# Attention's q and k stacks turned in one transpose per half and laid out by SBUF transfers, with the long fills spread over the steps

## The chip, the cores and the metric

One core of a Trainium2 chip. The metric is the device time of one execution in microseconds (us); smaller is better. Engines are named as in the profile: PE (matmul; PEld is its weight load), DVE, ACT, POOL, and SP, which here does little but issue DMA transfers from its queue.

## What is computed

A sandwich of two residual layers over x of shape (4, 1024, 256), f32:

```python
x = x + layernorm(attention(layernorm(x)))   # 16 heads of 16, rotary q and k, full softmax
x = x + layernorm(moe(layernorm(x)))         # 8 experts of width 684, 2 per token, silu gating
```

In attention q and k are projected, get a bias and rotary embedding, and `softmax(q k^T / 4) v` goes through an output projection. In the second layer each token goes to two of eight experts, chosen by its distance to eight centroids.

## The kernel before, in words

**Order of the work.** Attention is cut into 4 batches (b) x 4 groups of four heads (g) x 2 halves of 512 queries (qb): 32 units of 8 key blocks, 256 *steps* in all. A step (`step`, L720) takes one key block of one unit: the scores of four heads (`sc`, L737), less the rows' maxima by a second matmul into the same bank (L744), exp on ACT (L748), and the product with v of the step before (`av`, L813). The maxima of a unit that comes up to 12 steps later are drawn beside it: `pm` matmuls (L655), each reduced on DVE (L659). Everything else (norms, projections, splits, stacks, output projections, the choice of experts) is cut into small `Work`s (from L402). A planner at build time keeps a clock for each of PE, DVE, ACT and POOL (`free`), places Works by due step where their stated costs fit ("P430 A550" is 430 ns of PE and 550 ns of ACT), at most two PE works a step. The order so made is fixed on PE, DVE, ACT and SP (`manual_schedule`), and POOL's is the program's. What an engine waits for stalls all that stands behind it.

**Stacks.** Scores need near-f32 accuracy from matmuls that take the narrower type fp32r. So a value is split into hi = fp32r(value) and lo = value - hi. The product of a head is one matmul over 64 rows: q holds [hi, lo, hi, lo], k holds [hi, lo, lo, hi], 16 rows each. For each group and each half of 512 tokens, `rotated` (L542, POOL) applies bias and rotary embedding to q and k; `split_up` (L566) writes the split with all four copies (per q and k: a cast, a subtraction, two copies); `stack` (L587) turns it: for each pair of heads and for q and k, four 128x128 transposes (L596) fill one PSUM bank (tile `ps`), and ACT copies it (L603) into the tile that the matmuls read. That is four banks a half and group, 128 in all. In the first group DVE does the second half's split and k's copies. All the first group's splits and stacks come before its maxima, and those before step 0 (end of `sandwich`). `plan_stacks` (L1028) gives the due steps; `all_maxima` (L1020) finishes a group's stacks before its first maxima.

**Fills.** Two DRAM areas are prepared during attention: `rows` (tokens by expert), filled with an empty pattern from the tile `empty` by 35 transfers of 1032 KB (L285), and `wall` (each expert's weights in one block), by 88 DRAM-to-DRAM transfers (L303 to L312). All are issued on SP's queue at the start, behind the first loads. `biases_by_chunk` (L229, due step 54) adds biases to `wall` through small tiles (`flat`, `lin`, `lined`). Settled tokens are scattered into `rows` by POOL from L1000, and the expert stage reads both (L1170, L1178). `resid` stores (L860) are on SP's queue as well.

In SP's instructions each transfer waits for the one eight before it, because there are eight completion semaphores in turn.

Of the kernel before, what the change touches and what calls it, by code (L numbers as in the profile page):

```python
# [8 lines left out]
F32 = mybir.dt.float32  # L9
# [48 lines left out]
def sandwich(  # L58
# [22 lines left out]
    def bank(name, pool=ps1):  # L81
        return pool.tile([P, TB], F32, tag="bank", name=name)
# [155 lines left out]
    def biases_by_chunk():  # L238

        yield "P200 A400 W5000"  # L240
        pc = bank("plin", pssc)
        n = NE * NF
        for i in range(2):
            nc.tensor.transpose(pc[:n, i * FP : (i + 1) * FP], natural[:, i, :], ident[:FP, :FP])
        flat = cl.tile([n, 2, FP], F32, tag="eq", name="flat")
        nc.scalar.copy(flat, pc[:n, : 2 * FP].rearrange("p (i f) -> p i f", i=2))
        for i in range(2):
            nc.sync.dma_start(
                out=lin[i].rearrange("e (f p) -> (e f) p", p=FP), in_=flat[:, i, :]
            )  # L250
        lined = cl.tile([2 * NE, FF], F32, tag="oT", name="lined")
        nc.sync.dma_start(out=lined, in_=lin.rearrange("i e f -> (i e) f"))
        yield "P900 A800"
        pc = bank("pbias_", pssc).rearrange("p (f i) -> p f i", i=2 * NE)
        for f in range(NC + 1):
            m = P if f < NC else FR
            nc.tensor.transpose(
                pc[:m, f, :], lined[:, f * P : f * P + m], ident[: 2 * NE, : 2 * NE]
            )
        biases = cl.tile([P, NE, 2, NC + 1], F32, tag="gt", name="biases")  # L260
        pool.memset(biases, 0.0)
        for f in (slice(0, NC), slice(NC, NC + 1)):
            m = P if f.start < NC else FR
            nc.scalar.copy(
                biases[:m, :, :, f].rearrange("p e i f -> p i e f"),
                pc[:m, f, :].rearrange("p f (i e) -> p i e f", i=2),
            )
        nc.sync.dma_start(
            out=wall[:, :, OB:OR].rearrange("e p w -> p e w"),
            in_=biases.rearrange("p e i f -> p e (i f)"),  # L270
        )
# [7 lines left out]
    for i in range(NTS):  # L279
        nc.gpsimd.tensor_scalar(  # L280
            empty[:, :, i, C + 1], part_id.to_broadcast([P, NTB]), float(2 * B * T + i * P), None,
            ALU.add,
        )
    for i in range(NROW // (NTB * TS)):
        nc.sync.dma_start(  # L285
            out=rows[i * NTB * TS : (i + 1) * NTB * TS, :].rearrange(
                "(n i p) c -> p n i c", p=P, i=NTS
            ),
            in_=empty,
        )  # L290

    wall = tc.dram_tile([NE, P, WW], F32, name="wall")
    lin = tc.dram_tile([2, NE, FF], F32, name="lin")
# [3 lines left out]
    for e in range(NE):  # L297
        for w, to, cols in (
            (wg, 0, slice(0, FF)), (w1, FF, slice(FF - (P - R2), FF)), (w1, FF + P - R2, slice(0, NC * P))
        ):  # L300
            n = cols.stop - cols.start
            for k in range(KC):
                nc.sync.dma_start(  # L303
                    out=wall[e, :, k * WK + to : k * WK + to + n], in_=w[e, k * P : (k + 1) * P, cols]
                )
        nc.sync.dma_start(
            out=wall[e, :, O2:OB].rearrange("p (f c) -> p f c", f=NC),
            in_=w2[e, : NC * P].rearrange("(f p) c -> p f c", p=P),
        )
        for r in (0, R2):  # L310
            nc.sync.dma_start(out=wall[e, r : r + FR, OR:], in_=w2[e, NC * P :])
            nc.sync.dma_start(out=wall[e, r + FR : r + FR + 1, OR:], in_=b2[e : e + 1, :])  # L312
    token_id = const.tile([P, NTB], F32, tag="token_id", name="token_id")
    nc.gpsimd.tensor_scalar(token_id, tiles_at[:, :NTB], float(P), part_id, ALU.mult, ALU.add)

# [247 lines left out]
        e.tensor_tensor(flat, flat, sw.rearrange("p t h s d -> p (t h s d)"), ALU.add)  # L563
        return c

    def split_up(b, g, half, c, e):  # L566
        sp_ = ep2.tile([P, NTB, 2, 4, 4, HD], F32R, tag="split", name=f"split_{b}_{g}_{half}")
        for i in range(2):
            full = c[:, :, 4 * i : 4 * i + 4]
            at = lambda n: sp_[:, :, i, :, n, :]  # L570
            e.tensor_copy(at(0), full)
            e.tensor_tensor(at(1), full, at(0), ALU.subtract)
            e.tensor_copy(at(2), at(i))
            e.tensor_copy(at(3), at(1 - i))
        return sp_

    splits = {}

    def split(b, g, half, fast=False):

        e = nc.vector if fast and half else pool
        yield "G5500"
        c = rotated(b, g, half, e)
        yield "G4000"
        splits[b, g, half] = split_up(b, g, half, c, e)

    def stack(b, g, half, fast=False):  # L587

        for pr in range(2):
            for is_k in range(2):  # L590
                yield "P430 A550"
                if (half, pr, is_k) == (0, 0, 0):
                    stacks[b, g] = stack_tiles(b, g)
                ps = bank(f"ps_{b}_{g}_{pr}_{is_k}_{half}", pssc).bitcast(F32R)
                for t in range(NTB):
                    nc.tensor.transpose(  # L596
                        ps[:, t * P : (t + 1) * P],
                        splits[b, g, half][:, t, is_k, 2 * pr : 2 * pr + 2].rearrange(
                            "p h n d -> p (h n d)"
                        ),  # L600
                        ident_r,
                    )
                (nc.vector.tensor_copy if fast and is_k else nc.scalar.copy)(  # L603
                    stacks[b, g][pr][is_k][:, half * TB : (half + 1) * TB], ps
                )

    def stack_tiles(b, g):
        if (b, g) == groups[-1]:

            both = [  # L610
                ap1.tile([P, 2, T], F32R, tag=f"turned{pr}", name=f"stack_{b}_{g}_{pr}")
                for pr in range(2)
            ]
            return [[m[:, is_k] for is_k in range(2)] for m in both]
        return [
            [
                ap2.tile([P, T], F32R, tag=f"stack{i}", name=f"stack{i}_{b}_{g}_{pr}", bufs=6)
                for i in range(2)
            ]
            for pr in range(2)  # L620
        ]
# [98 lines left out]
    def step(n):  # L720
# [6 lines left out]
        if kb == 0:  # L727
            shifts[u].finish()
        es = []

        def scores(pr):
            q, k_ = stacks[b, g][pr]
# [74 lines left out]
    def weighted(u, kb, es):  # L807
        b, g, qb = order[u]
        if kb == 0:
            avs[u] = psav.tile([P, TB], F32, tag="av", name=f"av_{u}")  # L810
        av = avs[u]
        for j in range(4):
            nc.tensor.matmul(  # L813
                av[32 * j : 32 * j + 32, :], v_aug[kb][:, 4 * g + j, :], es[j],
                start=(kb == 0), stop=(kb == NT - 1),
            )
        free["P"] += 1200
        if kb == NT - 1:
            outputs(u, av)
# [200 lines left out]
    def all_maxima():  # L1020
        for u, (b, g, qb) in enumerate(order):
            for half in range(NQB):
                stacking[b, g, half].finish()
            yield from maxima(u)

    tops = all_maxima()

    def plan_stacks():  # L1028
        for k, (b, g) in enumerate(groups):
            for h in range(NQB):  # L1030
                deps = []
                if k:
                    deps.append(stacking[(*groups[k - 1], h)])
                if k == 1:
                    deps.append(Work(project(0, h, range(NTB), 1), -1))
                if g == 0 and b:
                    preparing[b, h] = Work(
                        prepare(b, h), drawing[b, g] - 22 + 6 * h,
                        after=[splitting[(*groups[k - 1], h)]]
                        + ([preparing[b, 0]] if h else []),  # L1040
                    )
                    deps.append(preparing[b, h])
                splitting[b, g, h] = Work(
                    split(b, g, h, fast=k == 0), drawing[b, g] - (16 if g == NG - 1 else 6), after=deps
                )
            for h in range(NQB):


                deps = [splitting[b, g, i] for i in range(NQB) if i == h or k == len(groups) - 1]
                stacking[b, g, h] = Work(  # L1050
                    stack(b, g, h, fast=k == 0), drawing[b, g] - 1,
                    after=deps + ([stacking[b, g, 0]] if h else []),
                    start=(k - 2) * ITS if 2 < k < len(groups) - 1 else 0,
                )
# [278 lines left out]
    with tc.manual_schedule(engines={ET.SP, ET.PE, ET.DVE, ET.Activation}):  # L1333
# [34 lines left out]
                    first = Work(first_tiles(), n, after=[settling[divmod(NA - 1, NQB)]])  # L1368
        while waiting:
            weighted(*waiting.pop(0))  # L1370
        backs[-1].finish()
        first.finish()
        make_room()
# [128 lines left out]
```

## Time and profile before

| | us |
|---|---|
| median of 3 runs | 1696.88 (1693.59 to 1699.7) |
| the profiled execution | 1706.47, its span 1704.7 |
| first transposes of stacks (L596) | at 36.5 |
| first maxima (L655) | at 42.4 |
| step 0 (first `sc`) | at 84.0 |
| last exp of attention (L748) | at 1079.1 |
| PE waiting for POOL's split, whole run | 16.8, longest 9.1 |
| granted PE clock, mean | 0.969 of full |

A line of the page names engine, operation, output<-inputs, shape and count, then busy time. Where one row stands for a tile, three numbers are the lowest, median and highest duration in ns. PE's times are pipelined and their ends modelled: a busy PE need not be at its peak. In the SP rows a duration is that of the issuing instruction, not of the transfer.

### The profile page before, as it was taken

Reading aid. Unit: us, or ns where it says so; the run is one execution under the profiler, and the core shown is the slowest. Engines: PE = TensorE matmul, PEld = TensorE weight load, DVE = VectorE, ACT = ScalarE, POOL = GpSimd, SP = SyncE. Lnnn points to the kernel's source line nnn. Section 1 sums busy time; section 2 is a strip of 40 time slices with the busy share of each in tenths; the row PEclk is TensorE's granted clock in tenths of the full one; section 3 lists DMA queues with packets and bytes.
Section 4 is the critical chain, followed back from the end, with each engine's and each line's share of the span. In section 5 each row is a group of like instructions: output and inputs, shape, how many; then the busy total and the mean of one; then the engine's idle time right before and its main releaser. Section 6 shows DMA issues by size and latency. Waiting matters only on the chain. (4 is left out here: it accounts for less than half of the span.)

```text
span 1704.7 us, 27788 instructions
## 1 busy us (share of the span) xinstructions
PE 1572.2 (92%) x9704; PEld 1028.0 (60%) x9704; DVE 1059.9 (62%) x2543; ACT 888.4 (52%) x1815; POOL 559.5 (33%) x1101
## 2 busy tenths in 40 slices
PE   3799999999999998999998999999999999999960
PEld 3454555654555554455554444688888888888850
DVE  6576788787788786778777786244334433333338
ACT  2266777676777776678676766522221111222213
POOL 5662344164393344475243121223131111111100
PEclk8999999999999999999999999999999999999985
DMA  8999810101000001000001013164455455777755
GB/s 247 302 300 254 227 45 6 36 26 38 1 26 13 26 13 51 1 26 14 22 5 38 1 38 128 59 217 176 169 209 193 164 208 217 256 282 282 285 202 212
DMA packets 92031, 213.77 MB, mean 125 GB/s; under 512 B 11469, under 2 KB 71092, under 8 KB 86004
## 3 DMA queue, kind: packets, MB, share of 16 engines
q1 hardware_dynamic: 81972, 182.49, 32.5%
q0 software_dynamic: 8768, 25.33, 4.4%
q10 hardware_dynamic: 1152, 4.19, 0.6%
q8 instruction: 76, 1.25, 0.3%
q14 instruction: 63, 0.52, 0.1%
HBM read 148.75 MB, written 80.58 MB: 135 GB/s over the span
## 5 line engine op out<-in xcount | busy, mean ns | idle before, releaser
L659 DVE TENSOR_REDUCE part<-pm 128x1 f32<-128x512 f32 x1024 | 642.0, 683 | 173.1 <-PE pm L655 158.9
L748 ACT ACTIVATE e<-sc 128x512 f32<-128x512 f32 x1024 | 530.3, 604 | 145.5 <-PE sc L744 136.2
L1210 PE MATMUL pu<-xT,w 128*128 128x256 f32 (+3 forms) x2024 | 361.5, 332 | 4.2 <-DMA w<-wall 1.3
L1216 ACT ACTIVATE sil<-pu,w 128x256 f32<-128x256 f32 (+3 forms) x276 | 117.0, 424 | 431.4 <-PE pu L1210 400.5
L1210 PEld LDWEIGHTS pu<-xT,w 128*128 128x128 f32 (+1 forms) x2024 | 313.8, 189 | 37.2 <-issue 5.1
L655 PE MATMUL pm<-stack,stack 64*128 64x512 f32 x960 | 276.7, 466 | 16.6 <-DVE part L659 13.7
L813 PE MATMUL av<-e,v 128*32 128x512 f32 x2048 | 277.5, 614 | 0.0
L744 PE MATMUL sc<-shift,bring 64*128 64x512 f32 x1024 | 232.1, 403 | 3.0 <-ACT shift L644 2.9
L1221 DVE SCALAR_TENSOR_TENSOR h<-pu,w,sil 128x256 f32<-128x256 f32 (+1 forms) x230 | 97.1, 423 | 218.5 <-ACT sil L1216 212.5
L737 PE MATMUL sc<-stack,stack 64*128 64x512 f32 x960 | 221.9, 411 | 5.4 <-issue 3.5
L655 PEld LDWEIGHTS pm<-stack,stack 64*128 64x128 f32 x960 | 133.3, 186 | 136.8 <-DVE part L659 87.2
L1257 POOL DMA_INDIRECT res<-yo,ids x71 | 68.7, 968 | 411.4 <-DVE yo L1256 409.0
L1244 PE MATMUL pe<-w,h 128*128 128x256 f32 x710 | 169.6, 386 | 0.0
L1244 PEld LDWEIGHTS pe<-w,h 128*128 128x128 f32 x710 | 131.0, 190 | 31.2 <-issue 15.2
L737 PEld LDWEIGHTS sc<-stack,stack 64*128 64x128 f32 x960 | 116.6, 187 | 37.6 <-ACT stack L603 8.4
L744 PEld LDWEIGHTS sc<-shift,bring 64*128 64x128 f32 x1024 | 111.4, 188 | 22.4 <-ACT shift L644 7.5
L603 ACT CAST stack<-ps 128x512 fp32r<-128x512 f32 x124 | 72.6, 593 | 47.5 <-PE ps L596 43.9
L596 PEld LDWEIGHTS ps<-ident_r,split 128*128 128x128 f32 x512 | 53.1, 145 | 72.7 <-ACT e L748 31.0
L1256 DVE TENSOR_SCALAR yo<-pe,xt 128x256 f32<-128x256 f32 x71 | 34.3, 484 | 100.3 <-PE pe L1244 100.3
L596 PE MATMUL ps<-ident_r,split 128*128 128x128 f32 x512 | 69.9, 268 | 16.8 <-POOL split L326 16.8
L1000 POOL DMA_INDIRECT rows<-xr,to x64 | 62.8, 981 | 68.3 <-DVE to L995 43.8
L813 PEld LDWEIGHTS av<-e,v 128*32 128x32 f32 x2048 | 40.5, 108 | 72.2 <-issue 69.6
(296 smaller groups left out, 1479.3 us busy)
## 6 DMA issues: line engine op xcount, KB each, us to landing
w<-wall SPq DMA_DIRECT2D x46, 2034.0 KB
rows<-empty SPq DMA_DIRECT2D x35, 1032.0 KB
xt<-rows SPq DMA_DIRECT2D x25, 258.0 KB
wall<-in_wg_dram SPq DMA_DIRECT2D x16, 342.0 KB
wall<-in_w_dram SPq DMA_DIRECT2D x16, 320.0 KB
wall<-in_w_dram SPq DMA_DIRECT2D x8, 640.0 KB
xb<-in_x_dram POOLq DMA_DIRECT2D x8, 512.0 KB
resid<-xb SPq DMA_DIRECT2D x8, 512.0 KB
```

Of the source, the lines that this page charges most:

```text
L596: nc.tensor.transpose(ps[:, t * P : (t + 1) * P], splits[b, g, half][:, t, is_k, 2 * pr : 2 * pr + 2].rearrange("p h n d -> p (h n d)"), i ...
L603: (nc.vector.tensor_copy if fast and is_k else nc.scalar.copy)(stacks[b, g][pr][is_k][:, half * TB : (half + 1) * TB], ps)
L655: nc.tensor.matmul(pm, q[r, t * P : (t + 1) * P], k_[r, half * TB : (half + 1) * TB], start=True, stop=True,)
L659: nc.vector.tensor_reduce(part[:, i, 2 * pr + s, half : half + 1], pm, AX.X, ALU.max)
L737: nc.tensor.matmul(sc, k_[r, kb * P : (kb + 1) * P], q[r, qb * TB : (qb + 1) * TB], start=True, stop=False,)
L744: nc.tensor.matmul(scs[s], bring[pr][r, :], shift[u][r, :], start=False, stop=True)
L748: nc.scalar.activation(e, scs[s], AF.Exp, scale=1.0 / HD**0.5)
L813: nc.tensor.matmul(av[32 * j : 32 * j + 32, :], v_aug[kb][:, 4 * g + j, :], es[j], start=(kb == 0), stop=(kb == NT - 1),)
L1210: nc.tensor.matmul(pu[:m, i, :n], w[:, c0 : c0 + m], xT[:, k, :n], start=(k == 0), stop=(k == KC - 1),)
L1216: nc.scalar.activation(sil[:m, :n], pu[:m, 0, :n], AF.Silu, bias=w[:m, OB + f : OB + f + 1])
L1221: nc.vector.scalar_tensor_tensor(h[:, f, :n], pu[:, 1, :n], bias, sil[:, :n], ALU.add, ALU.mult)
L1244: nc.tensor.matmul(po[:, :C], hs[j % 2][:, f, i * P : (i + 1) * P], w[:, O2 + f * C : O2 + (f + 1) * C], start=False, stop=(f == NC - 1),)
```

## The change

The split keeps only hi and lo of each of the eight heads (q's four, k's four), with one cast and one subtraction. One bank of four transposes turns q of all four heads of a half, another one k: two banks a half and group. The bank is copied to a new tile `ct` (four buffers), and 20 transfers inside SBUF on SP's queue bring its rows to their places in the two tiles of head pairs: for each head of q two of 32 rows x 512, for each head of k one of 32 rows and two of 16. A last piece of planned work, "W2600", stands for their latency, and stacks are due two steps sooner (drawing - 3). The planner moves its PE clock to where a group's stacks are ready before the first maxima. The long fills are put in a list and issued by the steps, one in each step to 36 and two after; `lined` uses another buffer.

```diff
-        lined = cl.tile([2 * NE, FF], F32, tag="oT", name="lined")
+        lined = cl.tile([2 * NE, FF], F32, tag="xr", name="lined")
...
-        nc.sync.dma_start(
-            out=rows[i * NTB * TS : (i + 1) * NTB * TS, :].rearrange(
+        bulk.append((
+            rows[i * NTB * TS : (i + 1) * NTB * TS, :].rearrange(
                 "(n i p) c -> p n i c", p=P, i=NTS
             ),
-            in_=empty,
-        )
+            empty,
+        ))
...
-    def split_up(b, g, half, c, e):
-        sp_ = ep2.tile([P, NTB, 2, 4, 4, HD], F32R, tag="split", name=f"split_{b}_{g}_{half}")
-        for i in range(2):
-            full = c[:, :, 4 * i : 4 * i + 4]
-            at = lambda n: sp_[:, :, i, :, n, :]
-            e.tensor_copy(at(0), full)
-            e.tensor_tensor(at(1), full, at(0), ALU.subtract)
-            e.tensor_copy(at(2), at(i))
-            e.tensor_copy(at(3), at(1 - i))
-        return sp_
...
-        yield "G4000"
-        splits[b, g, half] = split_up(b, g, half, c, e)
+        yield "G2100"
+        sp_ = ep2.tile([P, NTB, 8, 2, HD], F32R, tag="split", name=f"split_{b}_{g}_{half}")
+        hi, lo = (sp_[:, :, :, l, :] for l in range(2))
+        e.tensor_copy(hi, c)
+        e.tensor_tensor(lo, c, hi, ALU.subtract)
+        splits[b, g, half] = sp_
...
-        for pr in range(2):
-            for is_k in range(2):
...
+        for is_k in range(2):
+            yield "P430 A550"
+            if (half, is_k) == (0, 0):
+                stacks[b, g] = stack_tiles(b, g)
+            ps = bank(f"ps_{b}_{g}_{is_k}_{half}", pssc).bitcast(F32R)
+            for t in range(NTB):
+                nc.tensor.transpose(
+                    ps[:, t * P : (t + 1) * P],
+                    splits[b, g, half][:, t, 4 * is_k : 4 * is_k + 4].rearrange(
+                        "p h n d -> p (h n d)"
+                    ),
+                    ident_r,
+                )
+            ct = ep2.tile([P, TB], F32R, tag="ct", name=f"ct_{b}_{g}_{is_k}_{half}", bufs=4)
+            (nc.vector.tensor_copy if fast and is_k else nc.scalar.copy)(ct, ps)
+
+            parts = [(32, HD, HD), (48, 0, HD)] if is_k else [(32, 0, 32)]
+            for pr in range(2):
+                to = stacks[b, g][pr][is_k]
+                for s in range(2):
+                    for o, of, m in [(0, 0, 32)] + parts:
+                        r, f = 64 * s + o, 32 * (2 * pr + s) + of
+                        nc.sync.dma_start(
+                            out=to[r : r + m, half * TB : (half + 1) * TB].bitcast(F32),
+                            in_=ct[f : f + m, :].bitcast(F32),
+                        )
+        yield "W2600"
...
+        for _ in range(2 if n > 36 else 1):
+            if bulk:
+                to, of = bulk.pop(0)
+                nc.sync.dma_start(out=to, in_=of)
...
+                free["P"] = max(free["P"], stacking[b, g, half].ready)
...
-                    stack(b, g, h, fast=k == 0), drawing[b, g] - 1,
+                    stack(b, g, h, fast=k == 0), drawing[b, g] - 3,
...
+        for to, of in bulk:
+            nc.sync.dma_start(out=to, in_=of)
```

The transfers into `wall` are put in the list in the same way.

More of the change, by code (lines that the diff above doesn't have):

```diff
@@ L283, in sandwich @@
         )
+    bulk = []
     for i in range(NROW // (NTB * TS)):
-        nc.sync.dma_start(
-            out=rows[i * NTB * TS : (i + 1) * NTB * TS, :].rearrange(
+        bulk.append((
+            rows[i * NTB * TS : (i + 1) * NTB * TS, :].rearrange(
                 "(n i p) c -> p n i c", p=P, i=NTS
             ),
-            in_=empty,
-        )
+            empty,
+        ))
     wall = tc.dram_tile([NE, P, WW], F32, name="wall")
@@ L302, in sandwich @@
             for k in range(KC):
[L303 to L309, printed above, removed]
+                bulk.append((
+                    wall[e, :, k * WK + to : k * WK + to + n], w[e, k * P : (k + 1) * P, cols]
+                ))
+        bulk.append((
+            wall[e, :, O2:OB].rearrange("p (f c) -> p f c", f=NC),
+            w2[e, : NC * P].rearrange("(f p) c -> p f c", p=P),
+        ))
         for r in (0, R2):
-            nc.sync.dma_start(out=wall[e, r : r + FR, OR:], in_=w2[e, NC * P :])
-            nc.sync.dma_start(out=wall[e, r + FR : r + FR + 1, OR:], in_=b2[e : e + 1, :])
+            bulk.append((wall[e, r : r + FR, OR:], w2[e, NC * P :]))
+            bulk.append((wall[e, r + FR : r + FR + 1, OR:], b2[e : e + 1, :]))
     token_id = const.tile([P, NTB], F32, tag="token_id", name="token_id")
@@ L583, in split @@
         c = rotated(b, g, half, e)
-        yield "G4000"
-        splits[b, g, half] = split_up(b, g, half, c, e)
-    def stack(b, g, half, fast=False):
-        for pr in range(2):
-            for is_k in range(2):
[L591 to L604, printed above, removed]
-                )
+        yield "G2100"
```

## The prediction

> **What bounds the kernel now.** I read the page's shares and slices first, then the stages, then the first 50 us instruction by instruction, then SP's queue.
>
> ```profile
> PE 1572.2 (92%) x9704; PEld 1028.0 (60%) x9704; DVE 1059.9 (62%) x2543; ACT 888.4 (52%) x1815; POOL 559.5 (33%) x1101
> ...
> DMA  8999810101000001000001013164455455777755
> ```
>
> DMA is nearly saturated in the first five slices (213 us) and nearly idle in the rest of attention. Stage by stage (columns: stretch, its length, busy us and instructions of PE, PEld, DVE, ACT, POOL, granted clock, DMA share, GB/s):
>
> ```profile
> 219.00:500.00 281.00, 274.61 (x1873) 151.12 (x1871) 222.06 (x471) 209.44 (x420) 130.44 (x267) 1.00 0.08 23
> 500.00:930.00 430.00, 413.62 (x2779) 226.61 (x2780) 328.62 (x703) 308.75 (x619) 191.89 (x399) 0.99 0.07 21
> ```
>
> In attention PE shows 96 to 98%, DVE 76 to 79%, ACT 72 to 75%, POOL 45%. PE's ends are modelled, so I measured what a step is worth instead: on PE's timeline I took the time from one step's first `av` matmul to the next one's. The 251 steps average 3.95 us. The 60 with no extra work average 3.09; 49 that hold just one bank of stack transposes (L596, four of them) average 3.53. So a bank costs 0.44 us; a least-squares fit over all kinds of extra work gives 0.32 (plus or minus 0.07). On PE alone the four take 0.38 us (a bank begins at 89.70, the next matmul at 90.08). PE's order thus carries attention, with DVE close behind.
>
> The change touches these groups and this stretch of the start (PE's timeline: start, duration, line, operation):
>
> ```profile
> L603 ACT CAST stack<-ps x124: 564/587/647, 37.3 to 910.5; 128x512 fp32r<-128x512 f32 x124
> ...
> 36.50 0.75 PE L596 MATMUL ps<-ident_r,split 128*128 128x128 f32 x4 [9.09 <-POOL split L326]
> 38.71 3.79 PE L596 MATMUL ps<-ident_r,split 128*128 128x128 f32 x28 [1.46 <-POOL split L326]
> 42.42 0.79 PE L655 MATMUL pm<-stack,stack 64*128 64x512 f32 x2
> 43.15 2.01 PE L521 MATMUL pp<-wqk,nT 128*128 128x384 f32 x4
> ...
> 48.92 0.51 PE L655 MATMUL pm<-stack,stack 64*128 64x512 f32 x2
> ```
>
> PE waits for POOL's split, turns the first group, and starts maxima at 42.42. Nothing hides that chain: all later work stands behind it on PE. The fourth pair of maxima, the first to need everything of both halves of k, starts at 48.92.
>
> **Steady part: banks removed.** 128 banks become 64. By the instruction order of both builds, 114 of them lie inside steps before and 56 after; the rest stand ahead of step 0. So 58 banks leave the steps: at 0.38 us that is 22 us (0.32: 18.5; 0.44: 25.5). Each takes an ACT copy of 0.587 us along; that is in the measured worth of a bank. Two more banks leave the time before step 0, after the first maxima: 1 us.
>
> **POOL's split.** Per half and group two casts and four copies (0.398 us each) and two subtractions (0.736) become one cast and one subtraction of double width: 3.9 us become 2.3, some 50 us in all. POOL is 45% busy and PE waits for it 16.8 us in all, at the start: there the first bank needs the whole half now, at 34.32 + 0.80 + 1.47 = 36.6 against 36.50. No gain counted.
>
> **Added: 640 transfers.** Each half of a group gets 8 for q and 12 for k, on SP's queue. What does one cost SP? The nearest rows are the small ones out of SBUF and into 16 partitions (lowest, median, highest ns):
>
> ```profile
> L248 SPq DMA_DIRECT2D lin<-flat x2: 360/386/413, 272.4 to 272.9; - x2
> ...
> L127 SPq DMA_DIRECT2D wo<-in_wo_dram x16: 311/418/507, 3.9 to 15.5; - x16
> ...
> L311 SPq DMA_DIRECT2D wall<-in_w_dram x16: 797/804/1046, 145.3 to 218.3; - x16
> ```
>
> The dearest is the 44-row copy with both ends in DRAM, 0.80. I take 0.40 plus the 0.05 that lie between SP's issues at the start, 0.45; bounds 0.36 and 0.80. The second `lin` went out at 272.9 and what waits for it went on at 274.4: 1.5 us to land. 2 KB packets took 0.086 us on a DMA engine, so a transfer occupies one for under 0.2 us.
>
> A rule speaks against this: the Trainium skill, "DMA: Bandwidth & Descriptors", section "Rules for kernel authors", says to merge small transfers, since under 64 KB one pays mostly overhead; its section "Anatomy of one DMA" puts the fixed part at 2.0 us. These are 32 and 64 KB. Paid one after another, 40 transfers would be about 86 us before the fourth pair. But in the built order a transfer waits only for the one eight before it, so latency overlaps and the row's 0.45 us sets the pace: 18 us. I take the row.
>
> **At the start** nothing covers them. First transposes 36.6, copy to SBUF about 37.9, 40 transfers to 55.9, landed 57.4: the fourth pair is 8.5 us later than 48.92. The new PE order has one projection (1.5 us, L521) fewer ahead of that pair, so it still follows: 10 us. The waits also cool the clock. The rule in "TensorE: Matmul & The Clock Gate", section "Part 1: The HAM clock gate", drops it to half after an idle window of about 3.4 us; here a gap of only 1.64 us at 660.5 was followed by a projection of 3.51 us instead of 1.96. Two waits of some 6 us: by the rule's one window of 3.4 us at half rate 1.7 us lost, by the row up to 3.4. I take 2. Sum 12 us; with 0.36 an issue 8, with 0.80 some 26. A gain here is excluded: the transfers come after everything that the chain did before, bar 16 transposes (1.6 us, already in 42.42 against 36.6).
>
> **In the steps** the transfers are hidden: from a group's last transposes to its first maxima the new order leaves 7 steps for the second group, 10 or more for all others (39 us), against 18 + 1.5 us. If that cover went, up to 20 us a group. The buffers between (`ct`, four) make an ACT copy wait until the transfers of four copies ago have landed. This is tight only in steps 1 to 4, where the second group's transfers end about 100 to 107 us and ACT wants the buffers until about 111: nothing, or 10 us with dear issues. `resid` stores (L860) now stand ahead of stack transfers on SP and hold them until POOL's sums are done; the margin of 13 steps at those places covers that.
>
> **Waits.** PE gets 200 more semaphore instructions, ACT 230 (counted in the builds). They show 0.017 us each: 3.4 us on PE, mostly on the path. I take 3.
>
> **Fills moved.** SP's queue before:
>
> ```profile
> 15.93 0.67 SPq L303 DMA_DIRECT2D wall<-in_wg_dram  x1
> 16.72 119.69 SPq L285 DMA_DIRECT2D rows<-empty  x35
> ```
>
> 35 fills at 3.42 us become one a step (3.9 us), then two smaller ones a step; all done by step 80, while the first scatter into `rows` comes after step 64 and the first weight fetch at 1024 us. They wait for no engine, only for their place on SP, so they still fill the queue to about step 36: 120 us of fills and some 18 us of stack transfers in 142 us. Cost nothing: cover is the 14 to 18 steps those groups have. A gain: no load on the path was waited for between 16 and 100 us, so nothing either. `lined` now shares a buffer with the fills' source, which is free by step 36; it is wanted at 50. After 1080 us nothing changes.
>
> **Sum.** -22 - 1 + 12 + 3 = -8 us. The profiled execution took 1706.47 us (span 1704.7); it would become 1698. The median shown is 1696.88, 9.6 less; the same difference gives 1689.
>
> **Rivals.**
> - A larger gain: banks at 0.44 (25.5), issues at 0.36 (8 us), half the waits hidden: -25.5 - 1 + 8 + 1.5 = -17: 1680. For it: the bare-step comparison. Against: the fit's 0.32.
> - Slower by SP's issue price: the transfers have an address on both ends in SBUF as the 0.80 us row has both in DRAM. Start 26 us, ACT stalls in steps 1 to 4 another 10, waits 3, less 23: +16, 1713. It decides from about 0.65 us an issue. Against: every row with one end in SBUF is at 0.5 or less.
> - DVE takes the bound: bare steps at 3.09 us hold four reductions of 0.683 = 2.7 us plus other DVE work, so emptier steps stay at DVE's pace. A bank then brings 0.1 us, 6 us, against 15: 1706. Against: steps with a bank are measurably longer.
> - It doesn't do what it says: stack transfers sit behind 1 MB fills (3.4 us each, eight in flight: up to 27 us) and some group comes late once or twice: about 1700. Against: the margins.
>
> **Chances.** Main case 0.42, larger gain 0.18, issue price 0.23, DVE's pace 0.12, late stacks 0.05. A measurement of this kernel tells about 0.3%, 5 us, from no change. The main case has 6 us of spread around 1689, so 0.29 of it counts as faster and 0.13 as same; with the gain case faster is 0.47; same takes 0.03 of the late stacks: 0.16; slower 0.23 + 0.12 + 0.02 = 0.37. The range runs from 1674 (the gain case a little beyond its centre) to 1713, the issue-price case's centre; the likeliest case alone is 1682 to 1696.
>
> **What would show it.** Right: the fourth pair of maxima near 59 us and step 0 about 11 us later than 84; SP's issue near 0.4 us; steps without other work unchanged at 3.1 us and one-bank steps half as many; the end of attention about 8 us earlier; ACT's copies half as many; expert stage the same length. Wrong: issues of 0.6 us or more; PE or ACT waiting for stack transfers after step 7; one-bank steps not longer than bare ones; a fill landing in front of a stack that PE waits for.

## The result, and the profile after

The changed kernel takes 1742.93 us (median of 4 runs, 1742.09 to 1743.93) where the kernel before takes 1695.24 (4 runs): a ratio of 1.0281, 95% interval 1.0253 to 1.031. It is slower by 48 us; forecast were 8 us less, and the time lies above the whole range. The profiled execution took 1743.06 us, its span is 1741.3.

First the page's shares and slices, the same rows as before:

```profile
PE 1544.4 (89%) x9448; PEld 1003.6 (58%) x9448; DVE 1050.3 (60%) x2535; ACT 854.6 (49%) x1753; POOL 505.3 (29%) x915
...
DMA  2158987654521203212314003235445555678755
```

PE has 28 us less to do and is yet less busy in share. The DMA load of the first five slices has moved into slices 3 to 11. Then the two stretches of attention (columns as before):

```profile
219.00:500.00 281.00, 223.85 (x1488) 120.48 (x1486) 178.39 (x372) 163.30 (x331) 88.69 (x162) 0.90 0.61 166
500.00:930.00 430.00, 414.38 (x2773) 224.86 (x2770) 336.14 (x724) 307.15 (x619) 189.88 (x340) 0.99 0.22 55
```

The second is as it was; in the first PE does 51 us less in the same 281. So the loss has a place. To find it I took the step times again (first `av` of a step to the next step's; here step 0 stands for its first `av`), and cut the span where the two traces part:

| stretch (us) | before | after | difference | banks of stacks before, after |
|---|---|---|---|---|
| start to step 0's `av` | 88.7 | 108.5 | +19.8 | 14, 8 |
| steps 0 to 46 | 172.3 | 167.5 | -4.8 | 26, 12 |
| steps 46 to 54 | 29.4 | 84.5 | +55.1 | 7, 4 |
| steps 54 to 196 | 569.5 | 557.5 | -12.0 | 68, 36 |
| steps 196 to 255 | 220.1 | 198.0 | -22.1 | 13, 4 |
| rest (expert stage) | 624.6 | 625.4 | +0.8 | |

The sum, 36.8, is the difference of the two spans but for rounding. The profiled execution of before lies 11 us above its median, that of after on its median; the remaining 11 us up to 48 are in runs without a trace. So the table sets an execution of before that was 11 us longer than its median beside one of after that was not, and the rows after step 54 owe something to that, as the last part on the prediction shows.

What PE waited for (waiting tile, releaser, us in total, times, longest):

```profile
PE pbias__3345 L257 <- DMA lined<-lin: 47.1, 1, 47.1
PE ps L590 <- POOL split L328: 22.7, 4, 9.4
...
PE pm L660 <- DMA stack<-ct: 15.4, 6, 7.5
...
PE sc L746 <- ACT ct L598: 8.7, 6, 6.0
```

One wait of 47.1 us that before did not have is by itself as long as the difference of the medians. On PE's timeline it stands here:

```profile
294.59 0.55 PE L244 MATMUL plin<-ident,natural 114*48 114x114 f32 x2
...
347.06 0.72 PE L257 MATMUL pbias__3345<-ident,lined 16*128 16x16 f32 x6 [47.06 <-DMA lined<-lin]
```

Both belong to `biases_by_chunk`. The first makes `flat`, which goes by two small transfers to `lin` in DRAM and by a third back into `lined`; the second turns `lined`. `flat` was there at 295.2. When did its transfers leave? SP's queue:

```profile
331.51 7.50 SPq L606 DMA_DIRECT2D stack<-ct  x12
339.37 1.52 SPq L738 DMA_DIRECT2D wall<-in_w_dram  x2
341.00 0.88 SPq L248 DMA_DIRECT2D lin<-flat  x2
345.12 0.30 SPq L252 DMA_DIRECT2D lined<-lin  x1
345.52 0.61 SPq L606 DMA_DIRECT2D stack<-ct  x1
```

At 341, 46 us later. No row says that SP waited for PE or for `flat` in that time: from 295.2 to 341 it issued 32 stack transfers (pieces of 12, 8 and 12: 7.49 + 4.97 + 7.50 = 20 us) and 30 fills of `wall` (the other 24 us), all of which stood ahead. SP was simply that far behind the engines. Once issued, the three transfers took 6 us up to `pbias`.

Where SP fell behind is seen at the start of its queue (before, the fills began at 16.72):

```profile
14.67 1.34 SPq L127 DMA_DIRECT2D wo<-in_wo_dram  x3
37.37 78.44 SPq L606 DMA_DIRECT2D stack<-ct  x80
115.91 1.15 SPq L738 DMA_DIRECT2D rows<-empty  x2
...
232.75 34.85 SPq L738 DMA_DIRECT2D rows<-empty  x12
```

From 16 to 37 us SP issued nothing, and the first fill went out at 115.9, 99 us later than before. The 80 stack transfers ahead of it are those of the first two groups. SP issued them in two runs of 25 and 26 us; between these, from 62.7 to 89.7, it waited for ACT's copies of the second group, and the fills, which wait for nothing, waited behind. Later a fill that came alone took 0.58 us of SP, but in a run of twelve 2.9 us each (34.85 / 12). The price of an issue (lowest, median, highest ns), for stack transfers and, in another tile's answer, for the bias transfers:

```profile
L606 SPq DMA_DIRECT2D stack<-ct x640: 507/588/4192, 37.4 to 954.8; - x160
```

```profile
L248 SPq DMA_DIRECT2D lin<-flat x2: 401/409/417, 341.0 to 341.5; - x2
```

With the gaps between them 12 stack transfers take 7.50 us, 0.63 each; I had taken 0.45 from the `lin` row. And the start on PE's timeline:

```profile
35.98 2.27 PE L590 MATMUL ps<-ident_r,split 128*128 128x128 f32 x16 [9.39 <-POOL split L328]
45.72 0.79 PE L660 MATMUL pm<-stack,stack 64*128 64x512 f32 x1 [7.48 <-DMA stack<-ct]
...
58.47 0.76 PE L660 MATMUL pm<-stack,stack 64*128 64x512 f32 x1 [3.20 <-DMA stack<-ct]
...
63.91 1.03 PE L660 MATMUL pm<-stack,stack 64*128 64x512 f32 x2
```

The fourth pair of maxima, at 48.92 before and forecast for about 59, comes at 63.91: the first issue at 37.37, 40 x 0.63 and 1.5 to land give 64.1. A single maximum takes 0.76 us here where it took 0.50 before. The granted clock shows why (columns as above, clock third from the end; first after, then before):

```profile
44.00:53.00 9.00, 3.67 (x5) 1.64 (x6) 2.63 (x4) 0.00 (x0) 0.00 (x0) 0.50 0.32 73
...
44.00:53.00 9.00, 9.00 (x30) 4.05 (x28) 5.70 (x9) 2.04 (x5) 0.00 (x0) 0.99 1.09 308
```

With PE waiting between single maxima the clock stayed at half until 66.3 us; before, with PE busy throughout, it was full from 44.1 to 68.0.

### The profile page after: what moved, and what is told of

It reads as the page before. It is cut to its first block, busy times and chain, and to the rows that moved or that the text cites. A ratio compares the mean times of both kernels' runs of the same rounds, so it can differ in the third digit from the quotient of the medians.

```text
span 1741.3 us, 28175 instructions
## 1 busy us (share of the span) xinstructions
PE 1544.4 (89%) x9448; PEld 1003.6 (58%) x9448; DVE 1050.3 (60%) x2535; ACT 854.6 (49%) x1753; POOL 505.3 (29%) x915
## 3 DMA queue, kind: packets, MB, share of 16 engines
q10 hardware_dynamic: 1152, 4.19, 0.6%
## 5 line engine op out<-in xcount | busy, mean ns | idle before, releaser
L1220 PEld LDWEIGHTS pu<-xT,w 128*128 128x128 f32 (+1 forms) x2024 | 313.8, 189 | 36.5 <-issue 5.9
L753 PE MATMUL sc<-shift,bring 64*128 64x512 f32 x1024 | 224.8, 401 | 0.9 <-ACT shift L649 0.8
L746 PE MATMUL sc<-stack,stack 64*128 64x512 f32 x960 | 215.1, 409 | 9.2 <-ACT ct L598 8.7
L746 PEld LDWEIGHTS sc<-stack,stack 64*128 64x128 f32 x960 | 110.7, 187 | 39.9 <-ACT ct L598 15.1
L753 PEld LDWEIGHTS sc<-shift,bring 64*128 64x128 f32 x1024 | 107.3, 187 | 22.0 <-ACT shift L649 6.0
L328 POOL TENSOR_TENSOR rot<-turned,bias_qk 128x512 f32<-128x512 f32 x31 | 40.9, 1321 | 130.1 <-ACT turned L528 120.3
L523 PE MATMUL pp<-wqk,nT 128*128 128x512 f32 (+1 forms) x128 | 63.0, 617 | 0.0
L598 ACT CAST ct<-ps 128x512 fp32r<-128x512 f32 x62 | 36.7, 592 | 46.5 <-PE ps L590 34.4
```

The costliest lines, as they stand in the source:

```text
L523: nc.tensor.matmul(pp[:, :n], norm[b, h * 2 + t // 2][:, k, t % 2 * P : (t % 2 + 1) * P], wqk[:, k, g0:].rearrange("p g i h d -> p (g i h ...
L746: nc.tensor.matmul(sc, k_[r, kb * P : (kb + 1) * P], q[r, qb * TB : (qb + 1) * TB], start=True, stop=False,)
L753: nc.tensor.matmul(scs[s], bring[pr][r, :], shift[u][r, :], start=False, stop=True)
L1220: nc.tensor.matmul(pu[:m, i, :n], w[:, c0 : c0 + m], xT[:, k, :n], start=(k == 0), stop=(k == KC - 1),)
```

## The experiments

These rows gave a theory of three separate things. (1) `lined` waits because its transfers stand in SP's order behind stack transfers and fills that SP has not got through: 47 us. (2) The first group's 40 issues stand on the path: some 15 to 20 us. (3) The removed banks are worth what was forecast. Rivals are stated with each run. The runs were made on three other chips, on which the kernel before had medians of 1709.26, 1698.57 and 1693.30 us (called the second, third and fourth chip here; the first is that of the result above). So ratios are given, each to the kernel before on its own chip; even these compare less well from chip to chip than on one chip, as will be seen.

**Bias transfers on POOL's queue.** The three transfers of `biases_by_chunk`, nothing else; the order on PE, DVE and ACT stays the changed kernel's.

```diff
-            nc.sync.dma_start(
+            pool.dma_start(
                 out=lin[i].rearrange("e (f p) -> (e f) p", p=FP), in_=flat[:, i, :]
...
-        nc.sync.dma_start(out=lined, in_=lin.rearrange("i e f -> (i e) f"))
+        pool.dma_start(out=lined, in_=lin.rearrange("i e f -> (i e) f"))
```

> The changed kernel, with the two lin stores and the lined load issued on POOL's queue, not SP's. Theory (SP's queue): PE's one wait of 47 us for lined comes from those three transfers standing behind stack transfers and fills on SP; it goes, and with it some 3 us of cold clock: 1692 to 1699. Rival (DMA engines full): they land as late from another queue, 1735 or more. Rival (the next in line): PE now waits in the same place for the stacks of group (1,0) or for ct buffers, which are late on SP too: 1715 to 1730.

Measured on the second chip: 1.0104 (1.0085 to 1.0122), against 1.0281 on the first; the wait for `lined` is 2.2 us. So the DMA engines were not too full for these transfers, and `lined`'s new buffer, unchanged here, was free in time. Steps 46 to 54 fall from 84.5 to 42.0 us: the wait goes, and 42.5 us with it. But 42.0 is still 12.6 more than before, and the ratio lies between the theory (1692 to 1699, or 0.998 to 1.002) and the last rival (1715 to 1730, or 1.012 to 1.021). The same kernel once more, on the fourth chip:

> Only the bias transfers on POOL's queue, once more, beside the next kernel and the one with all three on one chip, since the first runs' chip and the second's gave different sums. My theory: the two losses add, so this one is about 14 us (0.8%) slower than with the first group by four banks as well: 1.0889 - 0.1 + 0.008, that is a ratio of about 0.997 (0.995 to 1.000). Rival (the loss at the start is given back or enlarged by a shift of all later work): 1.008 to 1.012 as in the first runs.

(The "1.0889" in it is a slip for 0.9889, the ratio of both parts undone.) Measured: 1.0056 (1.004 to 1.0073), between the two expectations; steps 46 to 54 take 43.3 us. Of what PE waits for there, two groups are left:

```profile
PE pm L660 <- DMA stack<-ct: 15.4, 6, 7.5
PE sc L746 <- ACT ct L598: 13.2, 8, 5.9
...
PE pbias__3345 L257 <- DMA lined<-lin: 0.8, 1, 0.8
```

The first is the start. The second is new against before, and 10.6 of its 13.2 us lie in steps 46 to 54: scores wait for ACT, which sits in its copy to `ct`, and that waits until older stack transfers have left the buffer. ACT's waits in the same run:

```profile
ACT ct L598 <- DMA stack<-ct: 14.1, 4, 7.3
```

This is SP's lateness again, by another way. The clock adds to it (steps 46 to 54 before, in the changed kernel and in this run):

```profile
261.10:290.50 29.40, 28.54 (x210) 15.51 (x209) 23.29 (x41) 22.36 (x45) 14.27 (x19) 1.00 0.04 5
276.00:360.50 84.50, 31.17 (x197) 15.65 (x196) 21.34 (x39) 20.49 (x42) 9.93 (x11) 0.66 0.59 158
276.80:320.10 43.30, 31.53 (x197) 15.25 (x197) 21.25 (x39) 20.18 (x42) 11.48 (x14) 0.88 0.70 187
```

PE has fewer matmuls to do and is busy 3 us longer. So taking `lined` off the queue removes the large wait and leaves the backlog.

**First group by four banks.** The first group alone is split and turned as before (four banks a half, no transfers); all others as in the changed kernel.

```diff
     def stack(b, g, half, fast=False):
+        if fast:
+            yield from four_banks(b, g, half)
+            return
```

> The changed kernel, but the first group is split and turned as before (four copies, four banks a half, no transfers). Theory (issue price at the start): step 0 comes back from 108.5 to about 89 us; the transfers of the second group start when they did, so SP's queue stays as late and the wait for lined keeps or gains a few us: 1724 to 1730. Rival (SP's whole backlog sets the end of that wait): the 20 us won at the start are given back there whole, 1740 or more.

Measured on the second chip: 1.0252 (1.0235 to 1.0269), step 0 at 94.2 us against 108.5, and the wait for `lined` 47.3 us as in the changed kernel. Once more, on the fourth:

> Only the first group by four banks, once more. My theory: the wait for lined stays at 47 us and is lost in full, 14 us come back at the start: a ratio of 1.014 to 1.018 where the changed kernel had 1.024 to 1.028. Rival: 1.024 to 1.028, the start's gain given back.

Measured: 1.0209 (1.0192 to 1.0226); step 0 at 89.5, `lined` 48.6. The start is won as the theory says, 14 and 19 us, and the wait for `lined` stays. Both totals lie between the theory (1.017 to 1.021, then 1.014 to 1.018) and the rival (over 1.026, then 1.024 to 1.028). The traces do not show the start's gain given back at `lined`: `flat` is there at 280.0 and 277.6 us, 15 and 18 earlier than in the changed kernel, `lin` leaves at 325.6 and 324.6, 15 and 16 earlier, and steps 46 to 54 take 83.0 and 86.2 us, against 84.5 and 81.2 in two profiles of the changed kernel. The whole queue moved forward with the start.

**Two queues for the first group.** 16 of the first group's 40 transfers on POOL's queue.

```diff
-                        nc.sync.dma_start(
+                        (pool if fast and o == 0 else nc.sync).dma_start(
```

> The changed kernel, with 16 of the first group's 40 transfers (the first 32 rows of each head) on POOL's queue. Theory (issue price of 0.65 us on one queue): the first maxima of k's second half come about 9 us sooner than at 58.5, 1743 falls by 6 to 10 us less what the later wait for lined takes back: 1734 to 1743, step 0 near 99. Rival (landing, not issue, sets it): step 0 stays at 108.

Measured on the second chip: 1.0288 (1.0271 to 1.0305). Step 0 comes at 98.3 us, 10 earlier than in the changed kernel: 16 issues fewer on SP at 0.63 are 10.1. That is the price of an issue, confirmed by taking issues away. In the total nothing of it is seen: the wait for `lined` is 47.4, and this run and the two above spent 570 to 576 us in steps 54 to 196 on this chip, where those two spent 559 and 557 on the fourth. Totals from this chip are therefore a weak measure beside those of others, the 1.0104 above among them; the waits and stretches carry the argument.

**Fills alone.** The kernel before, with only the fills in a list issued by the steps, and `lined` in its new buffer.

> The kernel before, with only the fills moved into the steps (and lined in the other buffer). Theory: the fills wait for no engine, so SP issues them at its own pace as before; the same time, 1690 to 1700. Rival (spreading the fills is itself what delays lined): a wait for lined of 10 us or more, 1705 or more.

Measured on the second chip: 1.0003 (0.999 to 1.0015), last step 2.6 us later than before, and no wait for `lined`. But this run did not spread the fills in time: those of `rows` left at 16.7 to 135.6 us, before at 16.7 to 133.0. SP does not wait for the steps; with nothing ahead of the fills it ran on at once. In the changed kernel they left at 115.9 to 288.9, for there stack transfers that wait for ACT stand ahead of them and between them. So the list alone costs nothing, and the fills are late only through the stack transfers among them. The stack transfers without the fills were not run.

**The changed kernel again**, as the mark for the third chip.

> The changed kernel itself, once more, as the mark for the others on this chip. Two readings of the first runs stand against each other. Chip: the two-queue kernel and the first-group-by-four-banks kernel won 10 and 14 us at step 0 and were no faster in ratio because their chip is harder on the changed kernel; then this run has a ratio of about 1.032 to 1.035. Given back: what is won at the start is lost again in later steps; then this run has 1.028 as on the first chip.

Measured: 1.024 (1.0223 to 1.0257), so neither reading: this chip is kinder to it than the first. It does not decide between them for the second chip, where the changed kernel itself was not run. The stretches of its trace agree with the table above within 3.3 us each.

**Both undone**, on the third chip: bias transfers on POOL's queue and the first group by four banks.

> Both undone together: the small bias transfers (lin, lined) on POOL's queue, and the first group by four banks and no transfers. My theory (two separate losses, 47 us of waiting for lined and 14 us at the start): steps 0 about +5 and 52 about +15 against before; the ratio falls from about 1.03 to 1.001 to 1.004. Rival (what is won at the start is given back later): as with the bias transfers alone, 1.009 to 1.012.

Measured: 0.9889 (0.9873 to 0.9906), 1679.18 us: 60 us less than the changed kernel beside it (1739.48), and faster than before. Both losses are removed in one kernel: against the changed kernel's trace on this chip step 0 comes 18.6 us earlier, and steps 46 to 54 are 44.7 us shorter (36.5, with 40 issues fewer in the queue). Better than expected: the expectation started from the 1.0104 of the second chip, and there these kernels lose more (the repeat above gave 1.0056).

**And 16 fills early.** The same, with 16 of the 35 fills of `rows` issued at 16 us, where SP is idle. In the kernel after it the bias transfers are left on SP's queue. Both ran on the third chip.

```diff
+    for _ in range(16):
+        to, of = bulk.pop(0)
+        nc.sync.dma_start(out=to, in_=of)
     token_id = const.tile([P, NTB], F32, tag="token_id", name="token_id")
```

> The same, and 16 of the 35 fills of rows issued at once in the start, where SP has nothing else to do (first group by four banks, so no stack transfer stands behind them). My theory: what is left at steps 46 to 52 (about 15 us: maxima and ACT's copies waiting for stack transfers that stand in SP's backlog) is backlog, and goes: step 52 within 3 us of before, ratio 0.992 to 0.997. Rival (the stacks are late of themselves, with their latency and the order of the steps): as the kernel without early fills, within 4 us.

> As the kernel before this one in the list, but the small bias transfers are left on SP's queue behind the stack transfers. My theory (the wait for lined is SP's backlog of fills and stack transfers together; 16 fewer fills of some 3 us each take 45 to 50 us off it): the wait for lined is under 5 us, and the time within 5 us of the kernel with them on POOL's queue. Rival (the transfers of the next group's stacks, 40 of them, stand ahead in any case and wait for ct): the wait stays over 20 us and the ratio is over 1.008.

Measured: with the bias transfers on POOL's queue 0.9866 (0.985 to 0.9883), 1674.56 us; left on SP's 0.9939 (0.9923 to 0.9956), 1687.41. The first is only 4.6 us faster than without early fills, hardly outside the rival's 4; what speaks for the theory is that steps 46 to 54 take 30.8 us where they took 36.5, and that step 52 comes 2.1 us later than in the kernel before, within the 3 expected. The second is the decisive one. Its bias transfers stand behind the very same stack transfers, and now leave at

```profile
284.75 1.00 SPq L248 DMA_DIRECT2D lin<-flat  x2
288.46 0.30 SPq L252 DMA_DIRECT2D lined<-lin  x1
```

and PE waits 12.1 us, not 47: with 16 fills of some 3 us taken out of SP's way, the wait is 35 us shorter. It is over the 5 us that I expected and under the rival's 20; the time, 12.9 us above that of the first, misses the 5 us too. So it is a backlog, worked off at some pace, and not a wait for the neighbouring transfers as such. In the first, PE waits 2.6 us for `lined` there, and in its whole run 2.7 for ACT's `ct` copies. The first once more, on the fourth chip:

> All three (16 early fills, bias transfers on POOL's queue, first group by four banks), once more, as the mark for these runs and to see whether it is faster than the kernel before on another chip: a ratio of 0.985 to 0.989. If the gain were of one chip alone: 0.993 to 1.000.

Measured: 0.9899 (0.9883 to 0.9916), 1675.97 us, a little short of the 0.985 to 0.989 expected. It beats the kernel before by more than the interval on two chips; beside the changed kernel it ran only on the third.

**A bank's price.** That kernel, on the fourth chip, and after each bank of every later group four more transposes into a bank that nobody reads.

> The kernel with 16 early fills (bias transfers on POOL's queue, first group by four banks), with the removed banks put back as idle work: after each bank of stacks of every later group another four transposes of the same data into a bank that nobody reads, 60 banks, without a copy. It leaves nothing out; it prices a bank. My theory (a bank on PE is worth 0.35 us, as steps 52 to 198 showed): 60 x 0.35 = 21 us slower than the kernel without them, 1695 where that has 1674.6. Rival (the banks cost little, and the gain came from the ACT copies that went with them, 0.59 us each, or from DVE and POOL): under 8 us.

Measured: 1748.25 us, 1.0312 (1.0284 to 1.034), 72 us more than without: neither. Sorted by what its steps hold, the 28 with one idle bank and no other work average 3.37 us, the 58 bare ones 2.96: 0.41 us for an idle bank, near the forecast's price. The other part is a side effect: the 26 steps with a real bank alone take 4.19 us where the kernel without idle banks has 3.44, and a new wait appears:

```profile
PE sc L796 <- ACT e L807: 28.7, 59, 0.5
```

An idle bank is drawn from the same few PSUM banks as the scores, so scores wait until exp has emptied theirs. As a price of all banks together the run is inconclusive; in the emptiest steps it gives 0.41.

## Why the prediction was wrong

- **"Fills moved ... Cost nothing", with `lined` "wanted at 50": the step that failed.** I asked when the *buffer* of `lined` is free, and whether each group's stack transfers land before its own first maxima. I did not ask what stands ahead of the bias transfers on SP's queue, though I listed their row as a price. They are three transfers with PE waiting at the end and no cover: 47.1 us, shown by moving them (42.5 us back) and by thinning the queue (35 us back).
- **"They still fill the queue to about step 36": failed with it.** My sum was 120 us of fills and 18 of stack transfers in 142 us of steps. In fact the first fill leaves 99 us later than before, and 100 stack transfers stand between the first fill of `rows` and the last, where 18 us at 0.45 count 40. "They wait for no engine" is true of the fills and not of their queue: the stack transfers ahead of them wait for ACT's copies. When `flat` was ready at about step 50, SP was 46 us behind.
- **"In the steps the transfers are hidden": failed in steps 46 to 54.** Scores wait for ACT's `ct` copies there, 6.0 us in the changed kernel, 7.3 and 10.6 with `lined` moved, and a clock below full adds about 3. They shrink to next to nothing (stretches of 30.8 and 34.2 us, with 2.6 and 5.4 of wait for `lined`) as the queue is relieved.
- **Start (+12): right in mechanism, the price of an issue mis-sized.** 0.63 us instead of 0.45 makes 25 us for 40 transfers instead of 18. I had kept 0.80 as the upper end and called 0.65 the deciding point; the rows that I took as nearest have one end in DRAM, and the row for SBUF on both ends was in no trace. The other side was right: latency overlapped, and 40 transfers took 25.3 us to issue, not the 86 of one after another. (The 2.0 us behind that 86 are given by the Trainium skill, "DMA: Bandwidth & Descriptors", section "Anatomy of one DMA", for transfers that GpSimd issues; these were SP's.) The fourth pair of maxima is 15.0 us later, step 0 19.8. In the 4.8 between, PE waits 8.7 us for POOL's split of the second group, where it waited 6.2, and has a half clock for longer; I had 2 for the clock and nothing more for that wait.
- **Banks removed (-22, and -1): right in size as far as it is shown.** 14 banks fewer in steps 0 to 46 for 4.8 us are 0.34 each; I had 0.38. In steps 54 to 196, which hold most of the banks, it stays open (see the late gain). The rival "DVE takes the bound" (0.1 a bank) falls. My comparison of steps in the prediction was off, though: counted again, before has 255 intervals of 3.89 us on average (not 251 of 3.95), and 42 with one bank alone average 3.42, 0.33 above the 59 bare ones at 3.09; the 0.44 was too high.
- **Waits (+3): not separable**; what they cost is contained in the worth of a bank that the stretches show.
- **Late gain, not forecast, and in part not the change's.** Steps 196 to 255 lost 22 us, of which 9 banks explain 3. Before, the clock was below full in much of this stretch (columns as above, clock third from the end):

```profile
915.00:970.00 55.00, 47.19 (x297) 22.98 (x299) 39.02 (x83) 32.01 (x68) 10.51 (x24) 0.90 0.05 18
970.00:1025.00 55.00, 51.84 (x338) 24.42 (x334) 46.62 (x112) 35.47 (x69) 12.39 (x28) 0.95 0.09 30
```

and after it was not:

```profile
968.00:1018.00 50.00, 47.07 (x325) 23.20 (x321) 42.77 (x95) 36.79 (x77) 10.38 (x27) 1.00 0.05 18
1018.00:1068.00 50.00, 48.17 (x333) 23.40 (x334) 44.98 (x106) 33.93 (x67) 11.59 (x24) 1.00 0.25 83
```

PE's waits for DVE's maxima there also went from 13.1 to 5.2 us. But the only other trace with the old stacks, the fills alone on the second chip, has stretches like those of before: 570.3 us in steps 54 to 196 and 220.3 in 196 to 255. On that same chip the kernels with the new stacks have 570 to 576 and 207 to 210. Like with like, then, 10 to 13 us of the late gain belong to the change, and the 12 us of steps 54 to 196, which would be 0.375 for each of 32 banks, are not seen there. On the other three chips kernels with the new stacks (the one with idle banks aside) have 556 to 559 and 198 to 199, and the old stacks have no trace. There only totals tell: with both losses undone and early fills the kernel is 24 and 17 us faster than before. Whether the late gain is the new order of the works or fewer ACT copies was not isolated.

By the two traces: +20 at the start, +55 in steps 46 to 54 (47 for `lined`, 6 for late `ct` copies, the rest mostly clock) and -38 for everything else, the long execution of before included, give the 36.8 us of the spans. Of the rivals, the one on the issue price had the start nearly right (26 us against 19.8) and put the stall at steps 1 to 4; the one on late stacks had the mechanism, a queue on which transfers stand behind fills, and gave it 11 us.

## What to carry to other kernels

A queue that issues in order is an engine with its own busy time: 640 transfers at 0.63 us are some 400 us of SP, and whatever else stands on the queue is late by its backlog, not by its own cost. A transfer that waits for an engine holds up all that stand behind it, also those that wait for nothing. When transfers are added or moved on a queue, list every *other* transfer on it that someone waits for without cover, and add up what stands ahead of it from the last moment at which the queue was empty. Work that needs nothing, like the fills, belongs in the queue's idle time at the start: 16 of them there took 35 us off one wait.

## What the hardware showed beside this

- The issue of a small transfer on SP depended on its two ends: 0.41 us from SBUF to DRAM (`lin`), 0.42 from DRAM into 16 rows (`wo`), 0.588 within SBUF; on POOL's queue the same transfers within SBUF took 0.498 (median of 16).
- The same two kernels (bias transfers on POOL's queue; first group by four banks) had spans 29 and 25 us longer on the second chip than on the fourth (1731.1 and 1702.1, 1751.7 and 1726.8), where the kernel before differed by 16 (medians of 1709.26 and 1693.30). A ratio to the kernel before does not take such a difference out whole.
